# A graph network with two mixtures of experts: rows sent to the experts carry the place and the weight of their result, and the experts scatter results to the tokens

## The chip, the core and the metric

The kernel runs on one core of one Trainium2 chip. A core has five engines that run side by side, each with its own queue of instructions in a fixed order: TensorE (PE, matrix products), VectorE (DVE), ScalarE (ACT), GpSimd (POOL) and SyncE (SP, which only issues transfers). They wait for each other through semaphores. Sixteen DMA engines move data between HBM and the on-chip memory; SP, ACT and POOL put transfers on their queues. A plain transfer may be issued from SP or ACT. A gather or a scatter whose row numbers are data is issued from POOL here; these are the indirect transfers.

The metric is the device time of one execution in microseconds (us). One execution was recorded by the hardware profiler; the times of three others stand beside it.

## The reference, cut to what matters

There are N = 6250 nodes with C = 256 features in fp32. Two layers follow each other. Each adds to x a graph aggregation and a second mixing term, and then a mixture of experts (MoE) on the normalized rows:

```python
# layer 0: x is (6250, 256); 32 experts, hidden 64, the best one only
xf = layernorm(x); logits = xf @ router_w.T + router_b
e = argmax(logits)
x = x + relu(relu(xf @ W1[e] + b1[e]) @ W2[e] + b2[e])

# layer 1: 16 experts, hidden 512, the best two
xf = layernorm(x); logits = xf @ gate_w + gate_b
v, e = top_k(logits, 2); w = softmax(v)
moe = sum_k w[k] * (relu(xf @ w1[e[k]] + b1[e[k]]) @ w2[e[k]] + b2[e[k]])
x = x + layernorm(xf + moe) * gamma + beta
```

The aggregations (over 100,000 edges, with a sort of the edges and a softmax over them in layer 1) are not touched by the change. They are most of the kernel's time.

## The kernel before

The 6250 rows are 49 tiles of 128 rows (NT = 49; the last has 106 rows, LAST). `xs`, an on-chip table of 128 x 49 x 256, holds x all along. The two mixtures are called f0 (layer 0) and f1 (layer 1). Each runs in three stages.

*Dispatch* (`dispatch`) goes through the tiles in chunks, of 7 tiles in f0 and of 4 in f1. `logits` normalizes the chunk's rows into `xn`, transposes them and computes the router's numbers on PE. `put` takes the best one or two experts on DVE (L364 and on), counts how many rows each expert has had so far, and so finds the row `pi` of a table in HBM, `xs_d`, where the row shall go. POOL scatters the normalized rows there (L398), one indirect transfer of 128 rows for each tile and each of its nk choices. Steps of the next chunk stand between those of the chunk before, in an order that a scheduler chooses. When all chunks are done, DVE computes from the experts' first tiles the row at which each token's result will stand (L453 to 467, `yi`). In f1 the normalized rows also go to a table of their own, `xn_d` (L347, ACT's queue), and the two softmax weights `wt` of all tokens are computed at the end (L1766 to 1771).

*Experts.* Each expert's rows in `xs_d` are cut into tiles of 128; 68 tiles in f0 and 107 in f1 hold rows with these inputs. The tiles behind a fixed number (64 and 104) lie in conditional blocks of 4 and 3 tiles. Which expert a tile belongs to and where its rows begin are register values that the queues load, so that one sequence serves all inputs. For each tile the weights are loaded (f1: `w1`, 512 KB, L1788, SP's queue; `w2` of all experts stays on chip), then the tile `xt` (f0: L930, ACT's queue; f1: L1791, SP's queue). PE transposes it (L131, `tr`), multiplies by the first weights (f1: `hT`, L1797), ACT and DVE share the relu (L1802, L1805), PE multiplies by the second weights (`y`, L1809), DVE adds the bias b2 (L1812) and the result is stored in the order of tiles to `ys_d` (f0: L942, ACT's queue; f1: L1813, SP's queue). `xt` has three buffers, `y` has three in f0 and two in f1. In f0 the experts run beside a sort of edges for layer 1, which uses DVE.

*The stage behind.* POOL gathers each token's result from `ys_d` by `pi` (`gather`, L300), one indirect transfer of 128 rows for each tile and choice. In f0 this is `normed` in `layer1_rows`: 49 gathers, and one DVE operation a tile adds the relu of the result to `xs` (L1066). In f1 it is the last stage of the kernel: seven chunks of 7 tiles. For each chunk the stored normalized rows come back (`xc`, L1827, ACT's queue), 14 gathered tiles are multiplied by their weights and added (L1832), the rows are normalized, multiplied by gamma (L1836), beta is added (L1837), x is added (L1838) and the rows are written out (L1841, SP's queue).

At the kernel's start a tile of zeros is written to the rows of `xs_d` and `ys_d` behind the used ones (`expert_slots`, SP's queue).

Of the kernel before, what the change touches and what calls it, by code (L numbers as in the profile page):

```python
# [8 lines left out]
F32 = mybir.dt.float32  # L9
# [43 lines left out]
def gps_kernel(ctx, tc, x, src, dst, edge_weight, g0_W, g0_b, m0_WqT, m0_WkvT, m0_WpT, m0_bp,  # L53
# [245 lines left out]
    def gather(o, tab, idx):  # L299
        nc.gpsimd.indirect_dma_start(  # L300
            out=o, out_offset=None, in_=tab,
            in_offset=bass.IndirectOffsetOnAxis(ap=idx, axis=0))
# [8 lines left out]
    def expert_slots(name, ne, nk):  # L311

        ns = (N * nk + ne * (P - 1)) // P
        rest = ns - N * nk // P
        xs_d = tc.dram_tile([ne * CAP + rest * P, C], F32, name=name + "_xs")
        ys_d = tc.dram_tile([ns * P, C], F32, name=name + "_ys")
        for d, j in [(xs_d, ne * CAP + j * P) for j in range(rest)] + \
                [(ys_d, j * P) for j in range(ns - rest, ns)]:
            nc.sync.dma_start(d[j:j + P, :], zero)
        return ns, xs_d, ys_d  # L320

    def dispatch(name, fb, fw, pps, ne, nk, bt, rw, rb, ns, xs_d, top, yi, finals, stored=None):

        mask = fb.tile([P, ne, bt + 1], F32, name="d_mask")
# [11 lines left out]
        kf = fb.tile([P, NT, nk], F32, name="d_kf")  # L338
        nc.vector.memset(kf[:, NT - 1, :], -1.0)

        def logits(t0):
            n = min(bt, NT - t0)
            finals(t0, n)
            xn = fw.tile([P, bt, C], F32, name="xn", bufs=3)
            layernorm(fw, xs[:, t0:t0 + n, :], xn, n)
            if stored is not None:
                nc.scalar.dma_start(stored[:, t0:t0 + n, :], xn[:, :n, :])  # L347
            lp = pps.tile([P, bt, ne], F32, name="lp")
            for i in range(n):
                xT = transposed(fw, pps, xn[:, i, :], "xT")  # L350
                for c in range(2):
                    nc.tensor.matmul(lp[:, i, :], xT[:, c, :], rw[:, c, :], start=c == 0, stop=c == 1)
# [5 lines left out]
        def put(t0, xn, lg, turn):  # L358
            n = min(bt, NT - t0)
            ti = fw.tile([P, bt, 8], U32, name="ti")  # L360
            full_ = n if t0 + n < NT else n - 1
            for i in range(n):
                r = rows(t0 + i)
                nc.vector.max(top[:r, t0 + i, :], lg[:r, i, :])  # L364
                nc.vector.max_index(ti[:r, i, :], top[:r, t0 + i, :], lg[:r, i, :])
            if full_:
                nc.vector.tensor_copy(kf[:, t0:t0 + full_, :], ti[:, :full_, :nk])
            if full_ < n:
                nc.vector.tensor_copy(kf[:LAST, NT - 1, :], ti[:LAST, full_, :nk])
# [3 lines left out]
                kf[:, t0:t0 + n, :, None].to_broadcast([P, n, nk, ne]), op=OP.is_equal)  # L373
# [20 lines left out]
            for i in range(n):  # L394
                t = t0 + i
                r = rows(t)
                for k in range(nk):
                    st = nc.gpsimd.indirect_dma_start(  # L398
                        out=xs_d, in_=xn[:r, i, :], in_offset=None,
# [45 lines left out]
        for e in range(0, ne, 8):  # L445
            q, eng = ((nc.sync, SP), (nc.scalar, ACT))[e // 8 % 2]
            for r in group_values(tail, e, eng, ne * CAP - P):
                st = q.dma_start(xs_d[ds(r, P), :], zero)
                tc.declare_no_dep(st.ins, group=name, reason="rows behind the tokens' ones")
                tc.add_to_no_dep_group(name, st.ins)  # L450

        sh = fb.tile([ne, ne], F32, name="d_sh")
        nc.vector.tensor_sub(gend, gend, gn[:, 0:1])  # L453
        nc.vector.tensor_scalar(gend, gend, float(P), None, op0=OP.mult)
        nc.vector.tensor_scalar(sh, ident[:ne, :ne], gend, None, op0=OP.mult)
        sp = pps.tile([P, ne], F32, name="lp")
        nc.tensor.matmul(sp, ones[:ne, :], sh, start=True, stop=True)
        ss = fb.tile([P, ne], F32, name="d_ss")
        nc.vector.scalar_tensor_tensor(ss, iota[:, :ne], -float(CAP), sp, op0=OP.mult, op1=OP.add)
        for k in range(nk):  # L460
            oh = fb.tile([P, NT, ne], F32, name="d_oh")
            nc.vector.tensor_tensor(oh, iota[:, None, :ne].to_broadcast([P, NT, ne]),
                                    kf[:, :, k:k + 1].to_broadcast([P, NT, ne]), op=OP.is_equal)
            nc.vector.tensor_tensor(oh, oh, ss[:, None, :].to_broadcast([P, NT, ne]), op=OP.mult)
            row_ = fb.tile([P, NT], F32, name="d_row")
            nc.vector.tensor_reduce(row_, oh, AX.X, OP.add)
            nc.vector.tensor_tensor(yi[:, k * NT:(k + 1) * NT], row_, pi[:, :, k], op=OP.add)
# [346 lines left out]
    zero = cst.tile([P, C], F32, name="zero")  # L814
    nc.vector.memset(zero, 0.0)
    slots_f0 = expert_slots("f0", 32, 1)
# [60 lines left out]
    def experts(name, ne, nk, hid, w1_d, b1_d, w2_d, b2_d, rw_d, rb_d, ns, xs_d, ys_d, finish, beside=None):  # L877
# [3 lines left out]
        with tc.tile_pool(name=name, bufs=1) as fp, tc.tile_pool(name=name + "w", bufs=2) as fw:  # L881
# [5 lines left out]
            top = fp.tile([P, NT, 8], F32, name="top")  # L887
            pi = fp.tile([P, nk * NT], I32, name="pi")
# [9 lines left out]
            with tc.tile_pool(name=name + "p", bufs=2, space=PSUM) as pps, \  # L898
# [4 lines left out]
                own, first, nt = dispatch(name, fb, fw, pps, ne, nk, CH, rw, rb, ns, xs_d, top, pi, finals)  # L903
# [4 lines left out]
            with tc.tile_pool(name=name + "q", bufs=2, space=PSUM) as pps, \  # L908
# [7 lines left out]
                def some(tiles):  # L916
                    for i in tiles:
# [11 lines left out]
                        xt = fv.tile([P, C], F32, name="xt")  # L929
                        nc.scalar.dma_start(xt, xs_d[ds(ar[j], P), :])  # L930
                        xT = transposed(fv, pps, xt, "xTt")
# [10 lines left out]
                        nc.scalar.dma_start(ys_d[i * P:(i + 1) * P, :], y)  # L942
# [8 lines left out]
            finish(fp, fw, pi, ys_d)  # L951
# [85 lines left out]
    def layer1_rows(fp, fw, pi, ys_d):  # L1037

        with tc.tile_pool(name="r1", bufs=1) as mp, tc.tile_pool(name="r1w", bufs=2) as mw, \
# [21 lines left out]
            def normed(t0):  # L1061
                n = min(4, NT - t0)
                for t in range(t0, t0 + n):
                    yg = mw.tile([P, C], F32, name="yg", bufs=8)
                    gather(yg, ys_d, pi[:, t:t + 1])
                    nc.vector.scalar_tensor_tensor(xs[:, t, :], yg, 0.0, xs[:, t, :],  # L1066
                                                   op0=OP.max, op1=OP.add)
# [646 lines left out]
    def expert_pairs(ne, nk, hid, w1_d, b1_d, w2_d, b2_d, rw_d, rb_d, ns, xs_d, ys_d):  # L1714
# [3 lines left out]
        xn_d = tc.dram_tile([NT * P, C], F32, name="xn1_d")  # L1718
        xn_t = xn_d.rearrange("(t p) c -> p t c", p=P)
        with ExitStack() as ctx1:  # L1720
            fp = ctx1.enter_context(tc.tile_pool(name="f1", bufs=1))
            wt = fp.tile([P, 2, NT], F32, name="wt")
            pi = fp.tile([P, nk * NT], I32, name="pi")
# [3 lines left out]
            b1T = fp.tile([P, ne * nf], F32, name="b1T")  # L1727
            with tc.tile_pool(name="f1w", bufs=1) as wp_:
# [5 lines left out]
                with tc.tile_pool(name="f1a", bufs=2) as fw, tc.tile_pool(name="f1b", bufs=1) as fb, \  # L1734
# [9 lines left out]
                    top = fb.tile([P, NT, 8], F32, name="top")  # L1744
                    nc.vector.memset(top[:, NT - 1, :], 0.0)
# [5 lines left out]
                    def finals(t0, n):  # L1751
                        for t in range(t0, t0 + n):
# [6 lines left out]
                    own, first, nt = dispatch("f1", fb, fw, pps, ne, nk, 4, rw, rb, ns, xs_d, top, pi,  # L1759
                                          finals, xn_t)  # L1760
# [4 lines left out]

                    df = fb.tile([P, NT], F32, name="df")  # L1766
                    nc.vector.tensor_sub(df, top[:, :, 1], top[:, :, 0])
                    nc.scalar.activation(df, df, AF.Exp)
                    nc.vector.tensor_scalar(wt[:, 0, :], df, 1.0, None, op0=OP.add)
                    nc.vector.reciprocal(wt[:, 0, :], wt[:, 0, :])  # L1770
                    nc.vector.tensor_mul(wt[:, 1, :], df, wt[:, 0, :])
                with tc.tile_pool(name="f1x", bufs=1) as fb, tc.tile_pool(name="f1v", bufs=2) as fv, \
# [3 lines left out]
                                                    ap=[[0, P], [1, ne * C]]))  # L1776
                    def some(tiles):
                        for i in tiles:
# [11 lines left out]
                            xt = fv.tile([P, C], F32, name="xt", bufs=3)  # L1790
                            nc.sync.dma_start(xt, xs_d[ds(ar[j], P), :])  # L1791
                            xT = transposed(fv, pps, xt, "xTt")
# [18 lines left out]
                            y = fv.tile([P, C], F32, name="y")  # L1811
# [75 lines left out]
```

## Time and profile before

| what | before |
|---|---|
| median of 3 runs | 4259.78 us (4258.5 to 4265.85) |
| the profiled execution | 4279.39 us |
| its span in the trace | 4277.6 us |
| mean granted PE clock over the span | 0.747 |
| busy: PE, DVE, ACT, POOL | 2514.4, 2102.2, 596.0, 1826.0 us |
| scatters to the experts (L398) | 147, busy 155.6 us |
| gathers of results (L300, `yg`) | 147, busy 168.3 us |

The span's stages, by the times at which their instructions run: layer 0 before its mixture to 1330 us; f0's dispatch 1330 to 1482; its experts 1482 to 1697; the rows of layer 1, with f0's gathers, 1697 to 1885; layer 1's edges to 3426; f1's dispatch 3426 to 3620; its experts 3620 to 4101; the last stage 4101 to 4278.

How to read it: busy time is the time in which an engine executes, so a stage can be long with no engine full, when each waits for another. In a row of a group, the first number is the busy time, the second the mean duration in ns, and what follows the second bar is the engine's idle time just before these instructions and which instruction ended most of it. The granted clock is the share of TensorE's full speed that the throttle allowed. An indirect transfer's time on POOL is the time in which POOL writes its descriptions; the data lands later.

### The profile page before, as it was taken

To read this page: it belongs to the slowest core of one execution; us is meant where nothing else is said; L and a number is where in the kernel's file an instruction comes from. 1 tells how busy PE (TensorE), PEld (TensorE's weight loads), DVE (VectorE), ACT (ScalarE), POOL (GpSimd) and SP (SyncE) were. 2 spreads that over 40 slices of the span, in tenths; PEclk is the share of its full clock that TensorE was granted. 3 is DMA by queue.
4 is the path that set the end of the run, shared out by engine and by line. 5 is a ranking of instruction groups with operands and counts; after the bars stand their busy time and mean duration, and the time that the engine had idled before them with its cause. 6 is when DMAs were issued, how large, how long until landed. Compare 5 with 4: busy or idle time off the path is not lost. (4 is left out here: it accounts for less than half of the span.)

```text
span 4277.6 us, 40881 instructions
## 1 busy us (share of the span) xinstructions
PE 2514.4 (59%) x10553; PEld 1822.0 (43%) x10553; DVE 2102.2 (49%) x6180; ACT 596.0 (14%) x1582; POOL 1826.0 (43%) x1864
## 2 busy tenths in 40 slices
PE   5455655677776487654554554555454444999920
PEld 4334444555555354531323333332233333888820
DVE  5345444445445666833544554554454654222247
ACT  3100000000001122221221221011010011222200
POOL 0566666566562400434445444544554245000046
PEclk9777877777786565777777777677786655999965
DMA  6643333233331344764433443454453163655644
GB/s 201 193 124 104 105 102 101 83 97 96 100 96 38 133 141 118 200 169 126 124 114 110 128 117 103 123 160 140 131 144 84 44 251 134 185 182 182 185 149 128
DMA packets 371451, 560.63 MB, mean 131 GB/s; under 512 B 106308, under 2 KB 259557, under 8 KB 370943
## 3 DMA queue, kind: packets, MB, share of 16 engines
q0 software_dynamic: 89760, 245.19, 20.5%
q1 hardware_dynamic: 243446, 273.73, 20.4%
q10 hardware_dynamic: 37992, 38.89, 2.8%
q8 instruction: 93, 1.52, 0.2%
q14 instruction: 160, 1.30, 0.1%
HBM read 440.48 MB, written 117.09 MB: 130 GB/s over the span
## 5 line engine op out<-in xcount | busy, mean ns | idle before, releaser
L300 POOL DMA_INDIRECT h<-h_d,idx x782 | 745.1, 953 | 814.2 <-DVE brk L1266 238.9
L300 POOL DMA_INDIRECT xg<-xw_d,idx x782 | 756.4, 967 | 550.0 <-issue 211.9
L1415 PE MATMUL ps<-w,S 128*128 128x260 f32 x1564 | 432.1, 438 | 374.4 <-DVE S L1410 256.7
L1415 PEld LDWEIGHTS ps<-w,S 128*128 128x128 f32 x1564 | 335.3, 219 | 488.5 <-DVE S L1410 281.8
L300 POOL DMA_INDIRECT yg<-f_ys,pi x147 | 168.3, 1145 | 813.1 <-SPq L1820 490.9
L802 PE MATMUL ps<-xg,S 128*128 128x256 f32 x1564 | 457.4, 439 | 81.2 <-DVE S L799 45.7
L802 PEld LDWEIGHTS ps<-xg,S 128*128 128x128 f32 x1564 | 333.4, 225 | 166.3 <-issue 59.1
L805 DVE SCALAR_TENSOR_TENSOR acc<-ps,in,acc 128x256 f32 x392 | 187.7, 479 | 387.6 <-remote 234.0
L1419 DVE SCALAR_TENSOR_TENSOR acc<-ps,in,acc 128x260 f32 x196 | 94.3, 481 | 556.6 <-remote 525.1
L1288 PE MATMUL p<-ST,hw 128*4 128x512 f32 x392 | 230.2, 700 | 178.9 <-DVE ST L1282 71.1
L398 POOL DMA_INDIRECT f_xs<-xn,d_pi x147 | 155.6, 1059 | 250.5 <-ACT xT L133 78.0
L799 DVE TENSOR_SCALAR S<-iota,lo,wt 128x128 f32<-128x128 f32 x782 | 242.9, 349 | 0.1
L1404 DVE TENSOR_TENSOR w<-h,exi 128x2048 f32<-128x2048 f32 x98 | 222.7, 2272 | 11.7 <-ACT exi L1379 11.7
L1809 PE MATMUL y<-w,h 128*128 x856 | 215.0, 392 | 11.2 <-ACT h L1802 10.1
L1797 PEld LDWEIGHTS hT<-xTt,w 128*128 128x128 f32 x1712 | 211.4, 194 | 6.1 <-ACT xTt L133 0.5
L1797 PE MATMUL hT<-xTt,w 128*128 128x128 f32 x1712 | 212.1, 277 | 0.2 <-ACT xTt L133 0.2
L1290 ACT COPY a<-p 4x512 f32<-4x512 f32 x196 | 111.3, 571 | 662.2 <-PE p L1288 272.3
L1805 DVE TENSOR_SCALAR h<-hT,b1T 128x128 f32<-128x128 f32 x214 | 74.8, 350 | 253.2 <-ACT h L1802 252.4
L1809 PEld LDWEIGHTS y<-w,h 128*128 128x128 f32 x856 | 149.0, 189 | 45.6 <-ACT h L1802 23.5
L1288 PEld LDWEIGHTS p<-ST,hw 128*4 128x4 f32 x392 | 24.1, 88 | 315.2 <-issue 147.7
L749 PE MATMUL ctx<-v,k 128*128 128x129 f32 (+1 forms) x196 | 44.2, 362 | 172.4 <-ACT v L747 118.2
L131 PE MATMUL tr<-ident,xt 128*128 128x128 f32 x350 | 84.7, 330 | 89.0 <-DMA xt<-f_xs 88.2
(344 smaller groups left out, 3979.3 us busy)
## 6 DMA issues: line engine op xcount, KB each, us to landing
w<-in_L_ffn_w SPq DMA_DIRECT2D x123, 512.0 KB
lob<-lob_d SPq DMA_DIRECT2D x97, 512.0 KB
xT<-xnT SPq DMA_DIRECT2D x196, 128.0 KB
xt<-f_xs SPq DMA_DIRECT2D x107, 128.0 KB
f_ys<-y SPq DMA_DIRECT2D x107, 128.0 KB
xnT<-xT SPq DMA_DIRECT2D x98, 128.0 KB
xg<-xw_d,idx POOLq DMA_INDIRECT x782
h<-h_d,idx POOLq DMA_INDIRECT x782
```

Of the source, the lines that this page charges most:

```text
L300: nc.gpsimd.indirect_dma_start(out=o, out_offset=None, in_=tab, in_offset=bass.IndirectOffsetOnAxis(ap=idx, axis=0))
L398: st = nc.gpsimd.indirect_dma_start(out=xs_d, in_=xn[:r, i, :], in_offset=None, out_offset=bass.IndirectOffsetOnAxis(ap=pi[:r, t, k:k + 1] ...
L799: nc.vector.tensor_scalar(S[:, i, :], iota, lo0[:, t:t + 1], wt0[:, t:t + 1], op0=OP.is_equal, op1=OP.mult)
L802: nc.tensor.matmul(ps, S[:, i, :], xg[:, i, :], start=i == 0, stop=i == n - 1)
L805: nc.vector.scalar_tensor_tensor(a, ps, m[:, b:b + 1], a, op0=OP.mult, op1=OP.add)
L1288: nc.tensor.matmul(p4[:, :w], hw, ST[:, j:j + w], start=True, stop=True)
L1290: nc.scalar.copy(a4[:, :w], p4[:, :w])
L1404: nc.vector.tensor_tensor(w8[:, :m, :C].rearrange("p i (k d) -> p i k d", k=4), hg[u // 8][:, :m, :C].rearrange("p i (k d) -> p i k d", k= ...
L1415: nc.tensor.matmul(ps, S[:, i, :], w8[:, i, :], start=i == 0, stop=i == m - 1)
L1419: nc.vector.scalar_tensor_tensor(a, ps, k[:, q:q + 1], a, op0=OP.mult, op1=OP.add)
L1797: nc.tensor.matmul(hT[:, f, :], w1[:, c, f * P:(f + 1) * P], xT[:, c, :], start=c == 0, stop=c == 1)
L1809: nc.tensor.matmul(yp, h[:, f, :], w2e[:, f * C:(f + 1) * C], start=f == 0, stop=f == nf - 1)
```

## The change

A row that goes to the experts gets longer: behind its 256 features stand, as raw integer bits, the row of the result table where this token's result belongs, and the softmax weight; in f1 also a factor, 1 for the first choice and 0 for the second. `xs_d` rows are 257 floats wide in f0 and 259 in f1. `xn` therefore has one copy for each choice (three buffers for the first, two for the second), and the weights are computed chunk by chunk in `put`. Rows that hold no token carry the number 1 << 20, which lies behind the table, and the scatter leaves them out.

`ys_d` now has a row for every token and choice, in the tokens' order. The experts' tiles no longer store `y` in the order of tiles: `give_back` scatters it from POOL to the rows that the tile itself carries. In f1 the tile's result is first multiplied by its weight, and the normalized row times the factor is added, so that the two results of a token sum to the normalized row plus the mixture. `xt` has five buffers in f0 and four in f1, `y` three in f1. The stages behind load whole blocks of `ys_d` from SP's queue (`results`). Beta is added to `xs` before f1's experts and not in the last stage, and gamma is loaded earlier. The zero fill of `ys_d`, the store of `xn_d`, the end of `dispatch`, and `pi`, `wt` and `top` over all tokens go.

The diff, cut to its core:

```diff
+        rw_ = C + 2 * nk - 1
+        xs_d = tc.dram_tile([ne * CAP + rest * P, rw_], F32, name=name + "_xs")
+        ys_d = tc.dram_tile([nk * NT * P, C], F32, name=name + "_ys")
...
+    def give_back(name, ys_d, xt, y):
+        st = nc.gpsimd.indirect_dma_start(
+            out=ys_d, in_=y, in_offset=None,
+            out_offset=bass.IndirectOffsetOnAxis(ap=xt.bitcast(I32)[:, C:C + 1], axis=0),
+            bounds_check=ys_d.shape[0] - 1, oob_is_err=False)
...
+    def results(t, ys_d, k, t0, n):
+        whole = n if t0 + n < NT else n - 1
+        if whole < n:
+            nc.vector.memset(t[:, whole, :], 0.0)
+        r0 = (k * NT + t0) * P
+        if whole:
+            nc.sync.dma_start(t[:, :whole, :], ys_d[r0:r0 + whole * P, :].rearrange(
+                "(t p) c -> p t c", p=P))
+        if whole < n:
+            nc.sync.dma_start(t[:LAST, whole, :], ys_d[r0 + whole * P:r0 + whole * P + LAST, :])
...
 # dispatch, logits
-            xn = fw.tile([P, bt, C], F32, name="xn", bufs=3)
-            layernorm(fw, xs[:, t0:t0 + n, :], xn, n)
-            if stored is not None:
-                nc.scalar.dma_start(stored[:, t0:t0 + n, :], xn[:, :n, :])
+            xn = [fw.tile([P, bt, rw_], F32, name=f"xn{k}", bufs=3 - k) for k in range(nk)]
+            layernorm(fw, xs[:, t0:t0 + n, :], xn[0][:, :, :C], n)
+            for k in range(nk):
+                if k:
+                    nc.scalar.copy(xn[k][:, :n, :C], xn[0][:, :n, :C])
+                nc.vector.tensor_copy(xn[k].bitcast(I32)[:, :n, C], ids[:, k, t0:t0 + n])
+                if nk == 2:
+                    nc.vector.memset(xn[k][:, :, C + 2], 1.0 - k)
...
 # dispatch, put
+            if nk == 2:
+                df = fw.tile([P, bt], F32, name="df")
...
+                        nc.vector.tensor_sub(df[:r, i0:i1], top[:r, i0:i1, 1], top[:r, i0:i1, 0])
+                nc.scalar.activation(df[:, :n], df[:, :n], AF.Exp)
+                den = fw.tile([P, bt], F32, name="den")
+                nc.vector.tensor_scalar(den[:, :n], df[:, :n], 1.0, None, op0=OP.add)
+                nc.vector.reciprocal(xn[0][:, :n, C + 1], den[:, :n])
+                nc.vector.tensor_mul(xn[1][:, :n, C + 1], df[:, :n], xn[0][:, :n, C + 1])
...
-                        out=xs_d, in_=xn[:r, i, :], in_offset=None,
+                        out=xs_d, in_=xn[k][:r, i, :], in_offset=None,
...
 # dispatch, its end
-            oh = fb.tile([P, NT, ne], F32, name="d_oh")
-            nc.vector.tensor_tensor(oh, iota[:, None, :ne].to_broadcast([P, NT, ne]),
-                                    kf[:, :, k:k + 1].to_broadcast([P, NT, ne]), op=OP.is_equal)
-            nc.vector.tensor_tensor(oh, oh, ss[:, None, :].to_broadcast([P, NT, ne]), op=OP.mult)
-            row_ = fb.tile([P, NT], F32, name="d_row")
-            nc.vector.tensor_reduce(row_, oh, AX.X, OP.add)
-            nc.vector.tensor_tensor(yi[:, k * NT:(k + 1) * NT], row_, pi[:, :, k], op=OP.add)
...
 # f0's experts
-                        xt = fv.tile([P, C], F32, name="xt")
+                        xt = fv.tile([P, xs_d.shape[1]], F32, name="xt", bufs=5)
...
-                        nc.scalar.dma_start(ys_d[i * P:(i + 1) * P, :], y)
+                        give_back(name, ys_d, xt, y)
...
 # layer1_rows, normed
-                for t in range(t0, t0 + n):
-                    yg = mw.tile([P, C], F32, name="yg", bufs=8)
-                    gather(yg, ys_d, pi[:, t:t + 1])
-                    nc.vector.scalar_tensor_tensor(xs[:, t, :], yg, 0.0, xs[:, t, :],
-                                                   op0=OP.max, op1=OP.add)
+                yg = mw.tile([P, 4, C], F32, name="yg")
+                results(yg, ys_d, 0, t0, n)
+                nc.vector.scalar_tensor_tensor(xs[:, t0:t0 + n, :], yg[:, :n, :], 0.0,
+                                               xs[:, t0:t0 + n, :], op0=OP.max, op1=OP.add)
...
 # f1's experts
+                    bet = spread(fb, f1_beta, "bet")
+                    for t0 in range(0, NT, CH):
+                        nc.vector.tensor_tensor(xs[:, t0:t0 + CH, :], xs[:, t0:t0 + CH, :],
+                                                bet[:, None, :].to_broadcast([P, CH, C]), op=OP.add)
...
-                            xt = fv.tile([P, C], F32, name="xt", bufs=3)
+                            xt = fv.tile([P, xs_d.shape[1]], F32, name="xt", bufs=4)
...
+                            xf = fv.tile([P, C], F32, name="xf")
+                            nc.scalar.activation(xf, xt[:, :C], AF.Copy, scale=xt[:, C + 2:C + 3])
...
-                            y = fv.tile([P, C], F32, name="y")
+                            y = fv.tile([P, C], F32, name="y", bufs=3)
                             nc.vector.tensor_tensor(y, yp, b2[:, ds(ey[j], C)], op=OP.add)
-                            nc.sync.dma_start(ys_d[i * P:(i + 1) * P, :], y)
+                            nc.vector.scalar_tensor_tensor(y, y, xt[:, C + 1:C + 2], xf,
+                                                           op0=OP.mult, op1=OP.add)
+                            give_back("f1", ys_d, xt, y)
...
 # the last stage
-                    nc.scalar.dma_start(xc, xn_t[:, t0:t0 + CH, :])
-                    for t in range(t0, t0 + CH):
-                        for k in range(nk):
-                            yg = fw.tile([P, C], F32, name="yg", bufs=6)
-                            gather(yg, ys_d, pi[:, k * NT + t:k * NT + t + 1])
-                            nc.vector.scalar_tensor_tensor(xc[:, t - t0, :], yg, wt[:, k, t:t + 1],
-                                                           xc[:, t - t0, :], op0=OP.mult, op1=OP.add)
+                    xc, yg = (fw.tile([P, CH, C], F32, name=q, bufs=3) for q in ("xc", "yg"))
+                    for k, q in enumerate((xc, yg)):
+                        results(q, ys_d, k, t0, CH)
+                    nc.vector.tensor_add(xc, xc, yg)
...
-                    nc.vector.tensor_tensor(yn, yn, bet[:, None, :].to_broadcast([P, CH, C]), op=OP.add)
```

## The prediction

> **What bounds the kernel now.** I read the page's 40 slices first, to see that no engine leads all through; then busy time by windows, one for each stage that the diff touches; then the waits and groups of the last two stages; last single instructions, for what one scatter and one load take. The windows' columns are window, length, busy time of PE, PEld, DVE, ACT, POOL, the granted clock, the DMA share and GB/s.
>
> ```profile
> 3430.00:3625.00 195.00, 81.64 (x360) 71.89 (x360) 106.18 (x514) 24.59 (x65) 102.91 (x98) 0.50 0.55 196
> 3625.00:3860.00 235.00, 216.47 (x1404) 191.28 (x1404) 58.92 (x159) 52.78 (x162) 0.00 (x0) 0.98 0.59 184
> 3860.00:4102.00 242.00, 214.44 (x1381) 189.38 (x1379) 60.79 (x162) 52.39 (x160) 0.00 (x0) 0.98 0.55 168
> 4102.00:4278.00 176.00, 0.00 (x0) 0.00 (x0) 119.80 (x273) 3.38 (x8) 117.27 (x98) 0.50 0.48 148
> ```
>
> The rows are the second layer's dispatch, its experts (two windows) and the last stage. The dispatch has no full engine: a chain of DVE, PE, ACT and POOL sets its pace. The experts are PE's: 430.9 of 477 us at full clock, with DVE at a quarter and POOL idle. In the last stage DVE and POOL share the time and wait for each other:
>
> ```profile
> L1832 DVE SCALAR_TENSOR_TENSOR xc<-yg,wt,xc 128x256 f32<-128x256 f32 x98 | 45.1, 477 | 48.1 <-DMA yg<-f_ys,pi 46.9 <-issue 1.1
> L1837 DVE TENSOR_TENSOR yn<-yn,bet 128x1792 f32<-128x1792 f32 x7 | 14.1, 2015 | 0.0
> ```
>
> 98 gathered tiles cost DVE 45.1 us of adds and 46.9 us of waits; 14.1 us goes to bet.
>
> ```profile
> PE tr L131 <- DMA xt<-f_xs: 53.0, 39, 21.0
> ```
>
> In the experts PE waits for the loaded tile 39 times, 53.0 us; 21.0 of it is the first, so 32 us is what the load costs in 107 tiles: 0.6 us for each of 53 pairs (PE works on tiles in pairs).
>
> ```profile
> 3506.22 0.96 POOL L398 DMA_INDIRECT f_xs<-xn,d_pi  x1 [0.30 <-issue]
> ...
> 3522.71 0.95 POOL L398 DMA_INDIRECT f_xs<-xn,d_pi  x1 [4.80 <-DVE d_pi L393]
> ```
>
> ```profile
> 3509.03 1.09 DVE L124 TENSOR_SCALAR xn<-xs,ln_mv,ln_rs 128x256 f32<-128x256 f32 x3 [2.18 <-DMA f_xs<-xn,d_pi]
> ```
>
> POOL spends 0.96 us on one scatter and 0.30 between two. The second of these views, DVE's, gives the landing: the scatter that began at 3506.22 was the last of a chunk and ended at 3507.18, and the write that waited for its buffer began at 3509.03, 1.85 us later.
>
> **The change part by part.** The sum is made against the profiled execution, 4279.39 us, and shifted to the median at the end.
>
> *First layer.* The dispatch (1330 to 1472, 16.4 us per chunk, of which POOL has 8.9) gets one id copy of about 0.15 us per chunk: +1. Its removed tail (three DVE operations of 1.79 us) lay under a sort step that waits for ACT until 1482: 0. The experts (1482 to 1697) move their y store from ACT's queue to POOL, which has no instruction there; ACT loses a head-of-line wait for y (19.2 us in 6 waits), but PE is busy 176 of the last 200 us at clock 0.63, so I take -5 (bounds -20, +10: a scatter that DVE's sort steps hold up reaches PE only after the ring of five tiles is used up). The stage behind it loads 13 blocks of 512 KB instead of 49 gathers; DVE never waited for those (POOL waited for DVE), so DVE's pace stays: -3 (bounds -13, +7). The zero fills of ys (48 of 128 KB at the start, SP) lie beside gathers that ran no slower with them: 0. Together -7.
>
> *Second dispatch.* Before, 16 scatters (two chunks) take 25.7 us: 20.8 of POOL and about 5 of waits, 12.85 per chunk. Afterwards each chunk of 4 tiles has on ACT a copy of 1024 columns (about 1.0), an Exp and a return to Sqrt, and on DVE an id copy and a memset per copy of the rows, a subtraction and three small operations, about 1.0 together. The second copy has two buffers. In the order of instructions its id copy for chunk c+2 stands, in 9 of 12 places, just ahead of the reduction that gives chunk c+1's rows. It waits for chunk c's scatters to have landed; queued behind it on DVE are those rows, and POOL waits for them. A chunk then takes 8 scatters of 1.26 minus one gap (9.8), 1.85 to land, 1.0 of DVE, 0.3 of issue: 13.0. The stores of xn (13, ACT's queue, 6.4 MB) and the DVE tail go, at 3607 to 3610 beside scatters that end at 3615: 0. With about 4 us for the later first chunk: +6, rounded to +8 for the scatters' wider rows. Bounds 0 and +45.
> Here a rule is weighed. The trace's table loads are
>
> ```profile
> L1183 ACT ACT_TABLE_LOAD x16 | 20.5, 1283 | 1.6 <-ACT w L1408 1.2 <-ACT a L1290 0.3
> ```
>
> so 1.28 us, two per chunk, 2.6 us. The Trainium skill ("ScalarE: Activation LUTs", What ACT_TABLE_LOAD costs) adds a drain of about 1.38 us to each switch: 5.3 us per chunk. ACT has 24.6 us of work in 195, so 2.6 lies in its idle time. By the rule, 2.7 us more between Sqrt, Exp and the weights that the scatters need would, if it all fell on the chain, give 12 x 2.7 = +32. I take the row, since it shows no idle time of that size ahead of these loads; the rule makes the upper bound.
>
> *Second experts.* Their y is written by POOL, which is idle: 107 of 0.96 us. ACT gets one scaled copy (about 0.4) and DVE one fused multiply-add (0.42 to 0.48) per tile. DVE has 119.7 of 477 us and gets 51, ACT 105.2 and gets 43: not bounds. Seven additions of bet (14.1 us) now stand on DVE ahead of the first tile's work; part lies under the first weights: +5 (bounds +3, +14).
> The wait that decides is new. A tile xt holds its result's row, so its buffer is free only when the scatter has landed; there are 4. SP's queue holds the next loads of w1 behind this wait. In PE's order the transposes of tiles come in pairs, and 6.4 us of matmuls (hT 2.0, y 2.0, the other half, transposes 0.4 each) lie between y of tile D-4 and the transpose of tile D. In that time must fit: DVE 0.42 + 0.42 and 0.2 of hand-over, POOL 0.3 + 0.96, the landing L, SP's issue 0.35, and the load, which no longer shares its time with w1, 2.2 (before, behind w1, 3.9: issued 3807.83, transposed 3811.75). That is 4.85 + L. With L = 1.85 the stall is 0.3 us per pair: 53 x 0.3 - 32 = -16. But that landing is from a stage at 196 GB/s in bursts; the skill ("DMA: Bandwidth & Descriptors", Latency and other measured facts) gives HBM's latency as 0.2 us on average and 2 us at high load, and counts it as most of the fixed cost. This speaks against the change: with L = 3.85 the stall is 2.3, and the sum 53 x 2.3 - 32 = +90. I choose L = 2.5, nearer to the row because the experts move less (168 to 184 GB/s) and their scatters go singly; what the scatter's test of rows against the table's end adds is in no row, and is in L's bounds: stall 0.95, 50 - 32 = +18. The last scatter costs 1.7 more than the last store. Together +25 (bounds -16, +106).
>
> *Last stage.* 176 us become: DVE 119.8 - 45.1 - 14.1 + 14.1 (one addition of 1792 columns per chunk, as long as bet's) = 74.7; POOL 0; DMA 98 x 128 KB of loads and 6.4 MB out, 19.2 MB. The nearest row for plain loads with rows of 1 KB is the start of the kernel:
>
> ```profile
> 60.00:130.00 70.00, 56.88 (x266) 43.35 (x264) 32.04 (x81) 31.17 (x93) 2.99 (x3) 0.99 0.71 229
> ```
>
> At 215 GB/s, between this and the dispatch's 196, it is 89 us; loads for later chunks stand before the outs of earlier ones in SP's order, so the loads run ahead. With 6 for the first load and 6 for the last chunk's end: 101. That is -75 (bounds -85, at DVE's own pace, and -38, at 150 GB/s).
>
> Sum: -7 + 8 + 25 - 75 = -49.
>
> **The rivals.**
> *The ring of four tiles stalls PE (slower).* At L = 4.5 us the stall is 2.95 per pair, 53 x 2.95 - 32 = +124 in place of +18: 4279 + 57 - 20 = 4317. It decides from the point where the steady part eats the other -67: 53 s - 32 = 67, s = 1.87 us, L = 3.4 us. For it: gathers of the last stage land 4 us after their end under load. Against: there many are in flight at once, here one or two.
> *The dispatch is serialised.* If 2.7 us per chunk, the drain of the rule or as much in other waits, falls on the chain between Exp and the scatters, the chunk takes 15.7 us and the stage +40 in place of +8: 4211 + 32 = 4243. For it: DVE's waits for the landed scatters and for Exp stand in the same order. Against: ACT's and PE's steps can run inside the wait for the landing, where today they are waits of their own.
> *The last stage gets half.* At 150 GB/s, or with outs blocking SP, 138 us: 4211 + 37 = 4248.
> *The change doesn't do what it says.* Were the loads still held back by something as slow as the gathers, only the costs remain (+26): 4286.
>
> **How the numbers follow.** The profiled execution is 19.6 us (0.46%) above the median of the runs; I take the same for the changed kernel: 4279.4 - 49 - 19.6 = 4211. What a measurement can tell from no change is about 0.2%, 8.5 us: faster is under 4251, slower over 4268. The likeliest case has 0.60 (own range 4170 to 4248), the ring 0.17 (4255 to 4360; 0.16 slower), the dispatch 0.09 (0.05 faster, 0.02 the same, 0.02 slower), half the gain 0.12 (0.10 faster, 0.01, 0.01), no gain 0.02 (slower). Faster 0.75, same 0.04, slower 0.21. The range 4170 to 4292 leaves out about 0.12 of the ring's chance above and 0.05 of the rest at both ends.
>
> **What would show it.** Right: no POOL work after the last expert, last stage near 100 us with DMA over 190 GB/s; PE's waits for xt in the experts between 16 and 90 us without the first; dispatch near 200 us with DVE's id copy waiting for the scatters; 26 more table loads. Wrong: PE's wait for xt near 1.9 us per pair or above (the ring), scatters waiting for the weights' DVE operations (the dispatch), DVE waiting for yg in the last stage through all chunks (half the gain), or experts longer though PE does not wait for xt, which none of these cases holds.

## The result, and the profile after

The changed kernel is slower: 4317.43 us median of four runs (4307.94 to 4335.37) against 4260.17 of before, a ratio of 1.0137 with a 95% interval of 1.0102 to 1.0172. The forecast was 4211 us. The rival of the ring of four tiles had 4317; that its number was met is chance in good part, since it put the whole difference into f1's experts, and the stages below share it.

The profiled execution took 4335.37 us, 56 us more than the one of before. Marks in both traces (first or last instruction of a kind) cut this difference into stages:

| stretch | before | after | difference | forecast |
|---|---|---|---|---|
| start to f0's last scatter to the experts | 1470.2 | 1471.6 | +1.4 | +1 |
| then to f0's first transposed tile | 26.5 | 34.5 | +8.0 | 0 |
| f0's first to last transposed tile | 195.1 | 217.0 | +21.9 | -5 |
| then to the first gather of layer 1's edges | 186.9 | 202.4 | +15.5 | -3 |
| then to f1's first scatter | 1573.2 | 1568.1 | -5.1 | 0 |
| f1's first to last scatter | 161.8 | 173.2 | +11.4 | +8 |
| then to f1's first transposed tile | 12.4 | 16.1 | +3.7 | +5 |
| then to f1's last y on PE | 474.0 | 546.9 | +72.9 | +20 |
| then to the end | 177.5 | 103.7 | -73.8 | -75 |

The windows of the changed kernel, with columns as before; the rows are f1's dispatch, its experts in two windows, and the last stage.

```profile
3470.00:3682.00 212.00, 79.67 (x358) 71.42 (x358) 107.63 (x602) 67.49 (x112) 103.86 (x98) 0.50 0.45 152
3682.00:3950.00 268.00, 217.53 (x1385) 190.01 (x1386) 93.75 (x216) 78.39 (x214) 51.30 (x52) 0.97 0.52 157
3950.00:4232.00 282.00, 223.36 (x1398) 194.97 (x1396) 87.92 (x218) 78.28 (x214) 53.78 (x55) 0.96 0.49 145
4232.00:4333.00 101.00, 0.00 (x0) 0.00 (x0) 78.32 (x177) 3.39 (x8) 0.40 (x1) 0.52 0.56 190
```

The last stage is what was forecast: no POOL, 78 us of DVE in 101, 190 GB/s. DVE waits for loaded results 14.9 us in all, 12.8 of them in one wait:

```profile
L1850 DVE TENSOR_TENSOR xc<-xc,yg 128x1792 f32<-128x1792 f32 x7 | 14.1, 2011 | 14.9 <-DMA yg<-f_ys 14.9
```

The experts' windows show the loss. PE has 440.9 us of work in 550, where it had 430.9 in 477; DVE is at a third (a quarter before), ACT and POOL lower. What PE waits for, and what SP's queue waits for, in that stage (total us, times, longest):

```profile
PE tr L131 <- DMA xt<-f_xs: 93.7, 46, 2.9
```

```profile
SPq L1810 <- DMA f_ys<-y,xt: 243.5, 98, 7.5
SPq L1807 <- PE hT L1818: 116.9, 40, 7.6
```

PE's waits for the tile went from 32.0 to 93.7 us, which is 61.7 of the 72.9 (another 5.4 lie behind the last transposed tile). L1810 loads xt: 98 of its 107 issues stood behind a scatter that had not landed. One such loop in the timeline (start, duration):

```profile
3894.96 0.42 DVE L1833 TENSOR_TENSOR y<-y,acc 128x256 f32<-128x256 f32 x1 [0.84 <-PE y L1830]
3895.42 0.48 DVE L1834 SCALAR_TENSOR_TENSOR y<-y,xt,xf 128x256 f32<-128x256 f32 x1
3896.18 0.98 POOL L326 DMA_INDIRECT f_ys<-y,xt  x1 [5.05 <-DVE y L1834]
3896.74 0.38 SPq L1807 DMA_DIRECT2D w<-in_L_ffn_w  x1
...
3900.99 0.02 SPq L1810 DMA_DIRECT2D xt<-f_xs  x1
...
3903.00 0.41 PE L131 MATMUL tr<-ident,xt 128*128 128x128 f32 x2 [2.45 <-DMA xt<-f_xs]
```

The scatter ends at 3897.16. SP has issued w1 before that, so the next load of xt waits for the landing alone. It is issued at 3900.99, 3.8 us behind the scatter's end, and the tile is transposed at 3903.00: the load took 2.0 us.

Is this the usual case? In the changed kernel's trace, 45 of PE's waits for xt can be followed from the scatter of the fourth tile before it to the transpose. In 30 of them the load is issued 2.9 to 3.8 us behind the scatter's end (3.5 at the median), and the transpose follows 2.2 us later. In 11 the times are the other way round: the scatter has landed early, w1 is issued late and just ahead of xt, and the load takes 2.7 to 4.0 us.

In f1's dispatch, ACT's copy of the rows and DVE's id copy both wait for landed scatters, as forecast for DVE's:

```profile
ACT xn L372 <- DMA f_xs<-xn,d_pi: 50.8, 9, 12.5
DVE xn L373 <- DMA f_xs<-xn,d_pi: 46.0, 10, 9.2
```

A part that no step of the forecast named is at the start of f0's experts. `dispatch` ends with 32 blocks of empty rows (L448 before, L492 now), written from two queues. In the timelines of SP and ACT, before:

```profile
1463.10 19.21 SPq L448 DMA_DIRECT2D f_xs<-zero  x16
```

```profile
1462.73 19.19 ACTq L448 DMA_DIRECT2D f_xs<-zero  x16
```

and in the changed kernel:

```profile
1463.18 26.29 SPq L492 DMA_DIRECT2D f_xs<-zero  x16
```

```profile
1463.78 25.18 ACTq L492 DMA_DIRECT2D f_xs<-zero  x16
```

The blocks grew by 0.4%, from 128.0 to 128.5 KB, and their issue by a third. The 4 MB of b2 and the first xt stand behind them on the same queues: b2 was issued at 1482.81 before and at 1491.62 now, the first xt at 1484.40 and 1495.38. The first transpose comes 8.0 us later behind the last scatter.

### The profile page after: what moved, and what is told of

The parts are those of the page before. It is cut to its first block, busy times and chain, and to the rows that moved or that the text cites. A ratio compares the mean times of both kernels' runs of the same rounds, so it can differ in the third digit from the quotient of the medians.

```text
span 4333.5 us, 41374 instructions
## 1 busy us (share of the span) xinstructions
PE 2536.0 (59%) x10549; PEld 1829.2 (42%) x10549; DVE 2120.5 (49%) x6251; ACT 704.7 (16%) x1744; POOL 1843.8 (43%) x1894
## 5 line engine op out<-in xcount | busy, mean ns | idle before, releaser
L326 POOL DMA_INDIRECT f_ys<-y,xt x175 | 179.8, 1028 | 640.7 <-DVE y L1834 418.3
L1830 PE MATMUL y<-w,h 128*128 x856 | 224.0, 402 | 7.6 <-ACT h L1823 4.9
L1225 PE MATMUL kv<-u 128*128 128x129 f32 (+1 forms) x196 | 50.0, 412 | 219.2 <-DVE u L1217 198.6
L1830 PEld LDWEIGHTS y<-w,h 128*128 128x128 f32 x856 | 149.3, 193 | 43.6 <-ACT h L1823 19.5
## 6 DMA issues: line engine op xcount, KB each, us to landing
xT<-xnT SPq DMA_DIRECT2D x196, 128.0 KB
xnT<-xT SPq DMA_DIRECT2D x98, 128.0 KB
xt<-f_xs ACTq DMA_DIRECT2D x68, 128.5 KB
```

Source lines behind the costliest of these rows:

```text
L326: st = nc.gpsimd.indirect_dma_start(out=ys_d, in_=y, in_offset=None, out_offset=bass.IndirectOffsetOnAxis(ap=xt.bitcast(I32)[:, C:C + 1], ...
L1830: nc.tensor.matmul(yp, h[:, f, :], w2e[:, f * C:(f + 1) * C], start=f == 0, stop=f == nf - 1)
```

## The experiments

The theory (A): tile buffers that are released by a scatter's landing hold up the loads, in f1 through SP's queue and in f0 through ACT's. The rival (B): the added work of ACT, DVE and the scatters per tile does. The runs were on several chips, on which the stages with gathers differ by some 15%, while f1's experts agree within 1%. So each kernel is compared by its ratio to the kernel before on its own chip, and stretches are compared where the chips agree or within one chip. "Stretch" is from the first to the last transposed tile; it is 535.0 us in f1 for the changed kernel (467.5 before) and 217.0 in f0 (195.1 before). On the chip of the first four experiments, `f0_xt12`, whose f1 is that of the changed kernel, has 531.9 in f1.

**f1's ring.**

```diff
-                            xt = fv.tile([P, xs_d.shape[1]], F32, name="xt", bufs=4)
+                            xt = fv.tile([P, xs_d.shape[1]], F32, name="xt", bufs=8)
```

> f1's xt has 8 buffers in place of 4; all else is the changed kernel. Theory A (the ring of four, released by the scatter's landing, stalls PE): a load no longer waits for a scatter, PE's waits for xt in f1's experts fall from 93.7 us to about 32 as before the change, the stage from 548 us to about 485, the kernel from 4317 to about 4255. Theory B (the added work of ACT and DVE per tile, or the scatters' traffic, delays PE): the waits and the stage stay within 15 us of 548, the kernel within 0.4% of 4317.

Measured: 3868.24 us, 1.0047 of before (1.0028 to 1.0066). Its transposes on PE, with the first and last start, and its waits on SP's queue:

```profile
L131 PE MATMUL tr<-ident,xt x214: 272/273/473, 3277.1 to 3753.6; 128*128 128x128 f32 x107
```

```profile
SPq L1807 <- PE hT L1818: 204.8, 57, 6.8
SPq L1807 <- PE tr L131: 108.2, 42, 5.6
```

The stretch is 476.5, 55 us less than in `f0_xt12` on this chip, and SP waits for PE to free w1 and no more for scatters. PE's waits for xt are 43.6 us. Theory A holds for most of the loss.

**The order of the two loads, with four buffers.**

```diff
-                            w1 = ...  ;  nc.sync.dma_start(w1, ...)
                             xt = ...  ;  nc.sync.dma_start(xt, ...)
+                            w1 = ...  ;  nc.sync.dma_start(w1, ...)
```

> f1's xt is loaded ahead of w1 of the same tile on SP's queue; four buffers as in the changed kernel. Theory A with its load term (the load of xt takes 3.7 us because 512 KB of w1 are issued just ahead of it): the stall per pair falls by the 1.5 us between 3.7 and 2.2, the stage by 53 x 1.5 = 80 at most and by 40 if w1, now behind the wait, is late in turn; the kernel 4240 to 4280. Theory A without it (the landing alone): the stage stays at 548 or gets longer, since w1 now waits for the scatter too.

Measured: 3920.59 us, 1.0177 (1.0158 to 1.0197).

```profile
L131 PE MATMUL tr<-ident,xt x214: 272/273/448, 3277.3 to 3807.1; 128*128 128x128 f32 x107
```

```profile
SPq L1807 <- DMA f_ys<-y,xt: 366.4, 98, 14.1
```

The stretch is 529.8, only 2 less. SP now waits 366 us for landings, and w1 stands behind that wait. The loads that PE waited for took 2.2 us at the median here and 2.3 in the changed kernel, so the new order had little to take away, and the 40 to 80 us expected of it did not come. While the ring is short, the landing holds the loop, and the order of the loads gains nothing.

**Both.** The edits of the last two together.

> Both: 8 buffers and xt ahead of w1. Theory A: neither the ring nor w1 holds the load, PE's waits for xt fall below 10 us, the stage to about 455 to 465, the kernel to about 4230. Theory B: within 15 us of 548.

Measured: 3828.82 us, 0.9951 (0.9931 to 0.9970).

```profile
L131 PE MATMUL tr<-ident,xt x214: 272/273/448, 3265.1 to 3705.6; 128*128 128x128 f32 x107
```

The stretch is 440.5, less than before the change, and behind the first tile PE has no wait for xt of any size. With the ring gone, w1 ahead of xt costs 36 us: in `f1_xt8` the loads that PE waited for took 3.9 us at the median. Rival B can own no more than the few us that are told with `before_first`, below.

**f0's ring.**

```diff
-                        xt = fv.tile([P, xs_d.shape[1]], F32, name="xt", bufs=5)
+                        xt = fv.tile([P, xs_d.shape[1]], F32, name="xt", bufs=12)
```

> f0's xt has 12 buffers in place of 5. Theory A for f0 (ACT, which issues the load of xt, waits in its order for a scatter's landing, and the relus of earlier tiles stand behind it): the transposes' stretch, 195 us before and 217 in the changed kernel, returns to about 195, the kernel to about 4295. Rival (the later start, 1506 in place of 1497, and the scatters' own time at POOL beside the sort make the delay): the stretch stays at 217 and the kernel at 4317.

Measured: 3928.88 us, 1.0200 (1.0171 to 1.0229). The first line is f0's transposes, the second the gathers of layer 1's edges:

```profile
L131 PE MATMUL tr<-ident,xt x136: 272/421/477, 1309.0 to 1497.9; 128*128 128x128 f32 x136
```

```profile
L300 POOL DMA_INDIRECT h<-h_d,idx x782: 940/946/1463, 1704.9 to 3023.1; - x196
```

The stretch is 188.9: theory A holds in f0. But the kernel gained nothing from it: its ratio is no lower than the 1.0177 of `f1_first` on the same chip, which has the changed kernel's f0. The edges took 1318 us from first to last gather; in f1_xt8, on the same chip, they began 23 us later and took 1291. So f1's dispatch began 1823 us after f0's last scatter, against 1819 there. The scheduler had put the edges' instructions on DVE and ACT in another order, though no line of them was changed. The next kernel asks whether that is the cause.

**Ten buffers in place of twelve.** The same edit with bufs=10.

> f0's xt has 10 buffers; the scheduler gives layer 1's edges an order on DVE that differs from the one in f0_xt12, as that differs from the changed kernel's. In f0_xt12 f0's transposes took 189 us in place of 216, but the edges (first to last gather) took 1318 in place of 1290, so that f1's dispatch began no earlier. Theory 1, the edges' time hangs on their order: here f0's stretch is 189 to 196 and the edges take something else than 1318, 1290 to 1300 if the order is a good one. Theory 2, something else sets the time at which the edges end, and an earlier start is always given back: the time from the last scatter of f0's dispatch to the first of f1's is the same as in f0_xt12, within 4 us.

Measured: 3907.92 us (3872.6 to 3910.94), 1.0108 (1.0050 to 1.0166).

```profile
L131 PE MATMUL tr<-ident,xt x136: 272/421/476, 1318.2 to 1504.5; 128*128 128x128 f32 x136
```

```profile
L300 POOL DMA_INDIRECT h<-h_d,idx x782: 941/947/1464, 1717.8 to 2995.9; - x196
```

f0's stretch is 186.3, the edges take 1278, and f1's dispatch begins 1793 us after f0's last scatter. This run was on another chip than f0_xt12, so by itself it decides nothing. Theory 2 falls on one chip: f1_xt8_first and f1_xt8 have the edges in the same order but for a few instructions; in the first they began 5 us earlier behind f0's last scatter, and f1's dispatch 9 us earlier. So an earlier start is not always given back. That the order makes the 27 us between 1291 and 1318 is likely and not shown: no run changed the order alone.

**The changed kernel again, and both rings mended.** `best` has f0's 12 buffers, f1's 8 and xt ahead of w1.

> The changed kernel as it is, beside the three others on their chip, so that their ratios to the kernel before can be set against its own. On the first chip its ratio was 1.0137; runs on another chip, on which the aggregations are shorter and the experts are not, point to 1.02 to 1.03 there.

> f0's xt has 12 buffers, f1's 8, and f1's xt is loaded ahead of w1. Theory A: both experts' stages lose what they lost alone (f0's transposes' stretch 189, f1's 440), the kernel is 3 to 3.5% faster than the changed one and 0.5 to 1.5% faster than before. Against: the two gains do not add, if layer 1's edges take over as the late part (their stretch was 28 us longer in f0_xt12).

Measured: the changed kernel 4313.52 us, 1.0130 (1.0082 to 1.0179), in line with its first ratio; its expectation of more was for faster chips, and this one was not. `best` 4202.45 us, 0.9866 (0.9811 to 0.9921), 2.6% faster than the changed kernel, with stretches of 186.4 in f0 and 438.4 in f1. The gain in f1 is whole. Of f0's, the edges take back 23 us again (1497 against 1474 from first to last gather, on one chip, in the order of f0_xt12): f1's dispatch begins 2007 us after f0's last scatter in both.

**The id copy in the dispatch.**

```diff
+                if k:
+                    nc.scalar.copy(xn[k].bitcast(I32)[:, :n, C], ids[:, k, t0:t0 + n])
+                    nc.scalar.copy(xn[k][:, :n, C + 2], zero[:, :n])
+                    continue
                 nc.vector.tensor_copy(xn[k].bitcast(I32)[:, :n, C], ids[:, k, t0:t0 + n])
```

> As best, and in the dispatches the second copy's numbers and factors are written by ACT, behind the copy of its rows, in place of DVE. Theory: DVE's wait for the landed scatters (46 us in 10 waits in the changed kernel) is what made f1's dispatch longer; the stretch of its scatters returns from 168 to 173 to about 160. Rival: Exp, table loads and the two buffers hold it wherever the copy stands; it stays at 168 or more.

Measured: 4203.47 us, 0.9879 (0.9833 to 0.9925), no different from `best`. The scatters of f1's dispatch, in `best` and then here:

```profile
L442 POOL DMA_INDIRECT f_xs<-xn,d_pi x98: 970/974/2026, 3462.4 to 3632.7; - x98
```

```profile
L446 POOL DMA_INDIRECT f_xs<-xn,d_pi x98: 968/974/2028, 3463.9 to 3624.8; - x98
```

170.3 became 160.9, as the theory had it: on this chip the wait on DVE was the dispatch's loss, and Exp with its table loads (21 in the stage) fits beside. The medians do not show the 9 us. Of the two profiled executions this one is 6 us shorter, though f0's last scatter came 7 us later in it, which nothing in the edit explains.

**Layer 1's rows from POOL's queue.** The loads of `results` in `normed` are issued by nc.gpsimd.

> As best_ids, and layer 1's rows load the results from POOL's queue, which is empty there, in place of SP's. Theory: the loads stand on SP behind stores that wait for DVE, and that made this stage about 10 us longer; it loses 5 to 12 us. Rival: the landing of the last scatter and the coarser blocks make it; within 3 us of best_ids.

Measured: 4180.40 us, 0.9831 (0.9783 to 0.9879). From f0's last transposed tile to the first gather of the edges it takes 195.1 us in place of 207.1, but f0's stretch is 196.1 in place of 188.3; together 4 us. DVE's waits for loaded results, 15.5 us in best_ids, are gone. But the scheduler also put the edges' instructions on DVE in another order again, that of the kernel before, so what the queue alone gives is not shown; the rest of the difference of the medians lies in other stages and is within their intervals.

**Without f0's part, and the kernel before with f1's loads mended.** In `f0_old`, f0's mixture is as before the change:

```diff
-        rw_ = C + 2 * nk - 1
+        rw_ = C + 3 if nk == 2 else C
...
-                        give_back(name, ys_d, xt, y)
+                        nc.scalar.dma_start(ys_d[i * P:(i + 1) * P, :], y)
...
-                results(yg, ys_d, 0, t0, n)
+                for t in range(t0, t0 + n):
+                    yg = mw.tile([P, C], F32, name="yg", bufs=8)
+                    gather(yg, ys_d, pi[:, t:t + 1])
```

`before_first` is the kernel before with f1's xt in 8 buffers ahead of w1.

> As best_ids, with the first mixture (f0) as before the change: rows of 256 floats, results stored in the tiles' order from ACT's queue, 49 gathers behind. Theory: f0's part of the change only costs; from the last scatter of f0's dispatch to the first gather of layer 1's edges it takes 408 us as before, in place of 423 to 428 with the deeper ring and 454 in the changed kernel, and the kernel is about 15 us faster than best_pool. Rival: the removed gathers gain something that the stage's other work now hides; 423 or more here.

> The kernel before the change, with f1's xt in 8 buffers and loaded ahead of w1. It tells how much of the gain of the mended kernels needs the change. Its waits for xt without the first were 32 us: the stretch of f1's transposes goes from 467.5 to about 435 and the kernel to 0.992 of before, if they were all due to w1 ahead of xt; if the store of y on the same queue holds the load back, less.

> best_pool once more, beside these two on their chip: ratio 0.978 to 0.988 to the kernel before, as measured, and about 15 us slower than f0_old if f0's part of the change only costs.

Measured, on one chip: `f0_old` 3778.11 us, 0.9803 (0.9760 to 0.9846); `before_first` 3818.14 us, 0.9903 (0.9869 to 0.9938); `best_pool` again (best_pool2) 3795.68 us, 0.9853 (0.9812 to 0.9894).

From f0's last scatter to the first gather of the edges `f0_old` takes 406.6 us and `best_pool` 414.6; the medians differ by 17.6. So f0's part of the change, with its ring mended, still costs some 8 us in this stretch. The start alone costs more: from the last scatter to the first transpose it takes 22.1 us in `f0_old` and 34.2 in `best_pool`, whose empty rows are the longer ones. The profiles of the two differ by 11.7 us over the whole span. The edges up to f1's dispatch add 6 to the 8, and f1 gives some back; the rest of the medians' difference is not resolved. `f0_old` is the fastest kernel here and beats both given ones.

`before_first` gains 1.0% without the change: its stretch in f1 is 432.2.

```profile
L131 PE MATMUL tr<-ident,xt x214: 272/273/478, 3201.2 to 3633.4; 128*128 128x128 f32 x107
```

Against its 432.2, `best_pool` and `f0_old` have 438.7 and 439.6 on the same chip: 6 to 8 us. That is all that is left for rival B, the added ACT and DVE work and the scatters in 107 tiles, and for the wider rows.

## Why the prediction was wrong, point by point

**The last stage.** Right: -75 forecast, -73.8 measured, by the stated mechanism.

**f1's steady part.** The mechanism was named, its size was wrong: +18 in the sum, 61.7 us of waits and 72.9 us in all measured. The step that failed is "I choose L = 2.5, nearer to the row": the landing was taken too short. In 30 of the 45 waits that can be followed, 3.5 us pass at the median from the scatter's end to the issue of the load. With it went the cover: PE's matmuls between the two tiles fill 5.6 us of such a loop, where the sum had 6.4. The load was not the fault in most loops: 2.2 us from its issue, where the sum had 0.35 and 2.2. In the 11 loops with a late w1 the sentence that the load "no longer shares its time with w1" fails too, and the load takes up to 4.0.

With these numbers the count comes out. Up to the scatter's end it is 2.2 us, then 3.5 to the issue and 2.2 to the transpose: 7.9 us against 5.6 of PE's work, a stall of 2.3 in such a loop. The other loops have less or none, so that a pair has 93.7 / 53 = 1.8 us, where the sum had 0.95. (The lower bound of the whole part, -16, left out the additions and the last scatter; with them it is -11.)

Of the two guides to L, the row of the dispatch (1.85) was the worse one. The estimate of 3.85, made with the 2 us at high load of the Trainium skill ("DMA: Bandwidth & Descriptors", Latency and other measured facts), lay nearer, though no trace here shows that latency by itself. Why the landing is longer here than in the dispatch stays open. In the loop shown, the 512 KB of w1 were issued 0.4 us before the scatter's end; no run took them away.

**The rival.** The point from which it decides was given as 1.87 us per pair, with the other terms at -67. The landing at which it was to decide, L = 3.4, is about what most of the waiting loops show. Over all pairs the stall came to 1.8, a little short of the point, and the kernel is slower all the same, because the first layer added to the loss. The rival's own 4317 needed +124 in this part, twice what came. So the ring alone does not explain 4317: mending it in f1 (f1_xt8) brings the kernel to 1.0047 of before, and not below 1.

**The first layer.** Forecast -7, measured +41.7 up to f1's first scatter. Three steps failed. The experts' -5 rested on ACT losing its head-of-line wait for y; the ring's wait took its place, on the queue of the engine that also does the relus: a stretch of 212 to 220 with 5 buffers, 184 to 196 with 10 or 12. The empty rows of the dispatch's end were not counted, though they are issued from the queues on which b2 and xt stand: +8. The rows' -3 rested on "DVE never waited for those"; now it waits for the loaded blocks, and the stage takes +15.5:

```profile
DVE xs L1092 <- DMA yg<-f_ys: 18.7, 5, 7.7
```

The loads stand on SP's queue among stores that wait for other engines. From POOL's queue, in best_pool, DVE does not wait, and the stage is 12 us shorter than in best_ids, with the reservation made there.

**The second dispatch.** +8 forecast, +11.4 measured, by the mechanism that was read from the order of instructions: best_ids, on a chip with the same times, removed it. The changed kernel's loads of Exp's table in this stage:

```profile
L409 ACT ACT_TABLE_LOAD x12 | 15.4, 1283 | 0.2
```

They take 1.28 us each, with 0.2 us of idle time ahead of all twelve. The drain that the Trainium skill ("ScalarE: Activation LUTs", What ACT_TABLE_LOAD costs) adds to a switch does not show there, and the +40 that was worked out with it did not come. But the case is not closed: on the chip of `f0_old` the same stretch is 152.4 and 151.0 with the moved copy (`f0_old`, best_pool2) and 134.8 in `before_first`, so there the dispatch costs 16 to 18 us more, and no run shows why.

**The additions of bet.** +5 forecast; the +3.7 ahead of f1's first transpose is near it by chance. That transpose waits for its load, not for the additions. The likely cause is the load's queue: it wrote 8 blocks of empty rows in 15.3 us, in place of 7.8, and so until 3673, after the last scatter, where before it had ended ahead of it. The additions run later, beside the first tiles:

```profile
3679.59 13.64 DVE L1793 TENSOR_TENSOR xs<-xs,bet 128x1792 f32<-128x1792 f32 x7 [14.77 <-DMA bet<-in_L_ffn_beta]
```

The first transpose began at 3682.87 and DVE's first relu at 3693.14, so what they cost lies in the row of the experts, and is not split off there.

## What to carry to other kernels

When a load's buffer comes to be released by a write at the end of the chain, write down the whole loop, from the result through the write's landing to the next load, and count what else is issued on the load's queue inside it; a ring that is too short costs its stall in every tile, and here four more buffers of 1 KB per partition took it away. Take the landing from many loops of a stage with like traffic, not from one line: here single landings lay between 1.5 and 4.3 us. Where a small load and a large one share a queue, put the small one, which is needed first, ahead; but only once it has no wait of its own, or the large one stands behind that wait. A change that helps one stage (here f1, where 98 gathers at the very end were on the path) need not be carried to another where the gathers lay beside other work.

## What the runs showed of the hardware

With rows of 1028 bytes in place of 1024 written to HBM, the issue of 16 blocks on each of two queues took 26.3 us in place of 19.2: 4.2 MB in both cases, so 160 GB/s in place of 218, if the issue keeps step with the transfers. On another chip it was 16.0 to 17.3 us with 1024 (before_first, f0_old) and 25.4 to 26.8 with 1028 (best_pool2). The length alone is not the rule: in f1, with rows of 1036 bytes, the 8 blocks of SP's queue took 15.3 us in place of 7.8 on the first chip, but 5.9 against 6.3 on that other one. What makes it was not tried.

In f1's experts of the changed kernel, a scatter of 128 rows of 1 KB had landed at the latest 1.5 to 4.3 us after POOL's end (2.9 at the median, by the issue of the load that waited), beside 145 to 157 GB/s of traffic; the one landing read in the dispatch took 1.85.

The same instructions took different times on different chips in the stages full of gathers and scatters, and the same in f1's experts, which PE and the ring bound. From the start to f0's first scatter the changed kernel took 1376 us in both of its profiles and its variants 1355 to 1365 on the chip of the second; on three other chips variants took 1181 to 1189. The scatters of f1's dispatch, with the code of before, took 161.8 us on the first chip and 134.8 on another (`before_first`), where POOL's own 98 times 0.96 and 0.30 us make 123. f1's experts with the ring of four differed by less than 1% (535.0, 533.2, 531.9, with f0_xt10's 536.4).
